# Layer 1's recurrent states two at a time: four row tiles for the spreads, four column tiles for the sums, the decay's second product on two row tiles

## The chip, the cores and the metric

The kernel runs on one core of one Trainium2 chip. The metric is the device time of one execution in microseconds. Two terms are used throughout. A *tile* of TensorE is a rectangle of its 128 by 128 array: a product with 32 input rows needs a row tile of 32 rows, a product with 32 output columns a column tile of 32 columns, and products on different tiles can be issued one right behind the other. A *bank* is a 128 by 512 f32 piece of PSUM, where matmuls leave their results.

## The reference

The input is 32 sequences of 64 tokens with 256 features, in f32. Four layers follow one another: layer 0 is a transformer block with self-attention and cross-attention, layer 1 a recurrent block, layer 2 two cross-attentions with 16 heads of 128 and a bias key and value, then an MLP, layer 3 a cross-attention and an MLP. The change concerns layer 1. It has 32 heads of 8 channels; each head keeps an 8 by 8 state, so that each of the 256 channels i has 8 states j:

```
w = exp(-exp(time_decay + tanh(xw @ td_w1) @ td_w2))     # td_w1: 256x64, td_w2: 64x256
r, k, v = xr @ Wr.T, xk @ Wk.T, xv @ Wv.T
for each token t:
    a      = k[t, i] * v[t, j]
    out[j] = sum over i of r[t, i] * (u[i] * a + s[i, j])
    s      = a + w[t, i] * s
```

What comes out is normalised head by head, multiplied by a gate, and passed through Wo onto the residual.

## The kernel before, in words

The 2048 tokens are cut into four groups g of 512 (8 sequences). Activations stand with features on the partitions: a work tile of `big` is 128 x 2 x 512, the 2 being the halves c of the 256 features. There are 12 such work tiles in rotation.

Each layer is a generator that yields between steps. `weave` runs one as the main thread and lets others advance at a given rate, and a scheduler orders each engine's instructions by priority, which follows the order in which the program issues them. Layer 1 of group 0 runs as the main thread, with layer 0 of group 1 and the precomputed keys and values of layer 2 (`keep`) beside it. Layer 1 of groups 1, 2 and 3 runs as the side thread of `layer2(0)`, `layer2(1)` and `layer2(2)`. In the profile, the state passes of the four groups lie at 313 to 418, 573 to 631, 1005 to 1063 and 1445 to 1501 us.

PSUM is divided in two pools. `bank` hands out 4 single banks. `banks` hands out 2 double banks (128 x 2 x 512, tag b2), which five users share: the spreads `vj`, layer 0's and 3's scores `sp` (L269), layer 2's scores `s2p` (L796), the mixing products `mp` (L488) and the group norm's `gm` and `gv` (L611, L617).

**The states.** The 16 states (c, j) of a group are done two j at a time in eight passes (c, n), where n stands for the states j0 and j0 + 2 with j0 = 0, 4, 1, 5. One pass is `states(c, n)`:

1. Spread (L558): a product with a 0/1 matrix, 32 rows to 128, copies v's channel j of each head to all 8 channels i. Two products, on row tiles m = j // 2, fill one double bank `vj`.
2. Multiply (L567, VectorE): a = vj * k, shifted by a token; GpSimd puts the starting state in front (L563).
3. Two scans (L573, VectorE): s = w * s + a along the tokens.
4. Multiply by r (L574, GpSimd).
5. Sums (L596): a product with another 0/1 matrix, 128 rows to 32 columns, adds up the 8 channels of each head, on two column tiles m of the bank `op`.

The list `ahead` keeps two passes in flight: pass at + 2 is started before the sums of pass at are issued. After the fourth pass of a half, `bp` (L603) adds the part with u. `gm` and `gv` then do the group norm, `og` (L618 to L627) the rest of it, and `al_d` the output product.

**The decay.** `dwp` (L165) multiplies xw by the 64 columns of td_w1, ScalarE takes the tanh on 64 partitions (L505), and two products `wp` (L510), one for each half c, read it; each is followed by two Exps on ScalarE.

`beside(i)` raises the priority of the second of two small products by 4000, so that the scheduler puts it right behind the first.

Names of other work that appears around the states: `al_o` (L331) is layer 2's output product and reads `o` (L836), which VectorE takes from the attention products `pv` (L825); `tp` (L810) are transposes of the softmax weights `pn` (L804, GpSimd); `q2p` (L165) are layer 2's queries; `x` (L344) is the residual; `nt_e` (L190) transposes the norm that follows layer 1's output product.

Of the kernel before, what the change touches and what calls it, by code (L numbers as in the profile page):

```python
# [10 lines left out]
AF = mybir.ActivationFunctionType  # L11
# [3 lines left out]
P = 128  # L15
# [6 lines left out]
NC = D // P  # L22
# [5 lines left out]
C_ID, C_HB, C_HB8, C_SEL, C_GAT, C_M0, C_M1 = 0, 128, 256, 384, 640, 704, 705  # L28
# [40 lines left out]
def kernel(  # L69
# [25 lines left out]
    def bank(name):  # L95
        return psum1.tile([P, 512], F32, tag="b1", name=name)

    def banks(name):
        return psum2.tile([P, 2, 512], F32, tag="b2", name=name)
# [17 lines left out]
    ct = cp.tile([P, C_N], F32, name="ct")  # L117
# [13 lines left out]
    def vec(name, i=0):  # L131
        at = VAT[name] + i
        return vt[:, at : at + 1]
# [27 lines left out]
    def linear(ps, w, at, step, y, cols=P):  # L161

        for kc in range(NC):
            o = at + kc * step
            PE.matmul(ps, w[:, o : o + cols], y[:, kc, :], start=(kc == 0), stop=(kc == NC - 1))  # L165
# [259 lines left out]
    @contextmanager  # L425
    def beside(i):

        if i:
            with tc.high_priority(offset=4000):
                yield  # L430
        else:
            yield
# [5 lines left out]
    def cbt(ap):  # L438

        return ap.rearrange("p c (b t) -> p (c b) t", b=GB)  # L440
# [7 lines left out]
    def layer1(g, work):  # L448
# [50 lines left out]
        yield  # L499
        yield  # L500
        de = big("de")
        dw = de[:64, 0, :]
        ps = bank(f"dwp_{g}")
        linear(ps[:64, :], w5, 384, 64, xw, cols=64)
        A.activation(dw, ps[:64, :], AF.Tanh)  # L505
        ws = big("ws")
        PL.memset(cbt(ws)[:, :, 0:1], 0.0)
        for c in range(NC):
            ps = bank(f"wp_{g}_{c}")
            PE.matmul(ps, w5[:64, 512 + c * P : 512 + (c + 1) * P], dw, start=True, stop=True)  # L510
            e = de[:, 1, :]
            A.activation(e, ps, AF.Exp, bias=vec("L1_xattn_time_decay", c))
            A.activation(bt(ws[:, c, :])[:, :, 1:], bt(e)[:, :, :-1], AF.Exp, scale=-1.0)
        yield

# [31 lines left out]
        yield  # L547
        k, v, r = made["k"], made["v"], made["r"]

        def states(c, n):  # L550

            j0 = (0, 4, 1, 5)[n]
            vj = banks(f"vj_{g}_{c}_{n}")
            for i in range(2):
                m, q = (j0 + 2 * i) // 2, j0 % 2
                rows = slice(32 * m, 32 * m + 32)
                with beside(i):
                    PE.matmul(  # L558
                        vj[:, i, :], ct[rows, C_SEL + q * P : C_SEL + (q + 1) * P], v[rows, c, :],
                        start=True, stop=True,  # L560
                    )
            a = big(f"a{c}{n}")
            PL.tensor_copy(  # L563
                a.rearrange("p i (b t) -> p i b t", b=GB)[:, :, :, 0:1],
                s0t[:, c, j0 : j0 + 3 : 2, g * GB : (g + 1) * GB].unsqueeze(3),
            )
            V.tensor_tensor(  # L567
                a.rearrange("p i (b t) -> p i b t", b=GB)[:, :, :, 1:],
                vj.rearrange("p i (b t) -> p i b t", b=GB)[:, :, :, :-1],
                bt(k[:, c, :])[:, :, :-1].unsqueeze(1).to_broadcast([P, 2, GB, S - 1]), ALU.mult,  # L570
            )
            for i in range(2):
                V.tensor_tensor_scan(a[:, i, :], ws[:, c, :], a[:, i, :], 0.0, ALU.mult, ALU.add)  # L573
            PL.tensor_tensor(a, a, r[:, c : c + 1, :].to_broadcast([P, 2, GT]), ALU.mult)  # L574
            return j0, a

        ruk = big("ruk")
        todo = [(c, n) for c in range(NC) for n in range(4)]
        ahead = [states(*todo[0])]
        yield  # L580
        ahead.append(states(*todo[1]))
        yield
        for c in range(NC):
            V.scalar_tensor_tensor(ruk[:, c, :], r[:, c, :], vec("L1_xattn_u", c), k[:, c, :], ALU.mult, ALU.mult)
        w9 = slot(L1_AT + 4)
        for at, (c, n) in enumerate(todo):
            if at + 2 < 8:
                ahead.append(states(*todo[at + 2]))
                yield
            if n == 0:  # L590
                op = bank(f"op_{g}_{c}")
            j0, a = ahead.pop(0)
            for i in range(2):
                m, q = (j0 + 2 * i) // 2, j0 % 2
                with beside(i):
                    PE.matmul(  # L596
                        op[32 * m : 32 * m + 32, :], ct[:, C_GAT + 32 * q : C_GAT + 32 * q + 32], a[:, i, :],
                        start=(q == 0), stop=(q == 1),
                    )
            yield  # L600
            if n == 3:
                bp = bank(f"bp_{g}_{c}")
                PE.matmul(bp, hb, ruk[:, c, :], start=True, stop=True)  # L603
                V.tensor_tensor(v[:, c, :], bp, v[:, c, :], ALU.mult)
                V.tensor_tensor(v[:, c, :], op, v[:, c, :], ALU.add)
                yield
# [390 lines left out]
def _layout(inputs):  # L997

    import numpy as np

    f = {k: np.asarray(v) for k, v in inputs.items()}
    i = np.arange(D)
    turned = (i // P) * P + (i % 16) * 8 + (i % P) // 16

    def rows(w):

        return w.reshape(-1, P, w.shape[1]).transpose(1, 0, 2).reshape(P, -1)

    def tall(w):

        return np.concatenate([w, np.zeros((P - w.shape[0], w.shape[1]), w.dtype)], 0)

    def slot(*parts):
        w = np.concatenate(parts, 1)
        return np.concatenate([w, np.zeros((P, WSLOT - w.shape[1]), w.dtype)], 1)

    l0 = {k[9:]: v for k, v in f.items() if k.startswith("L0_xattn_")}
    l1 = {k[9:]: v for k, v in f.items() if k.startswith("L1_xattn_")}
    l2 = {k[9:]: v for k, v in f.items() if k.startswith("L2_xattn_")}
    l3 = {k[9:]: v for k, v in f.items() if k.startswith("L3_xattn_")}  # L1020

    def mlp(w1, w2):

        return [slot(rows(w1[:, :512])), slot(rows(w1[:, 512:])), slot(rows(w2[:512])), slot(rows(w2[512:]))]

    qkv, kv = l0["w_qkv"], l0["w_kv"]
    w2 = l1["maa_w2"]
    maa_w1 = np.concatenate([l1["maa_w1"], l1["maa_w1"][:, 128:]], 1)
    slots = [
        slot(rows(qkv[:, :512])),  # L1030
        slot(rows(qkv[:, 512:]), rows(l0["w_ao"])),
        slot(rows(l0["w_q"]), rows(kv[:, :D])),
        slot(rows(kv[:, D:]), rows(l0["w_co"])),
        *mlp(l0["w1"], l0["w2"]),
        slot(rows(maa_w1), rows(l1["td_w1"]), tall(l1["td_w2"])),
        slot(w2[:4].reshape(P, D), tall(np.concatenate([w2[4], w2[4]], 0))),
        slot(rows(l1["Wk"].T), rows(l1["Wv"].T[:, turned])),
        slot(rows(l1["Wr"].T), rows(l1["Wg"].T[:, turned])),
        slot(rows(l1["Wo"].T[turned]), rows(l1["Wfk"].T)),
        slot(rows(l1["Wfr"].T), rows(l1["Wfv"].T)),  # L1040
    ]
    for a in "12":
        for q in range(4):
            at = slice(512 * q, 512 * q + 512)
            slots += [slot(rows(l2[n + a][:, at])) for n in ("wq", "wk", "wv")]
            slots.append(slot(rows(l2["wo" + a][at])))
    slots += mlp(l2["w_fc1"], l2["w_fc2"])
    slots += [
        slot(rows(l3["q_w"]), rows(l3["k_w"])),
        slot(rows(l3["v_w"]), rows(l3["cproj_w"])),  # L1050
        *mlp(l3["fc_w"], l3["proj_w"]),
    ]
    f["L1_xattn_gn_w"] = l1["gn_w"][turned]
    f["L1_xattn_gn_b"] = l1["gn_b"][turned]

    def feature_major(x):

        return x.reshape(G, GT, NC, P).transpose(3, 0, 2, 1)

    def token_major(x):  # L1060

        return x.reshape(G, TT, P, D).transpose(2, 0, 1, 3)

    ctx = f["ctx_2048"]
    arrays = {
        "x": token_major(f["x"]),
        "cT": feature_major(ctx),
        "s0": ctx[:, 2:10].reshape(B, NC, P, 8).transpose(2, 1, 3, 0),
        "m_self": f["mask_1x1xSxS2_fc1"].reshape(S, S),
        "m_cross": f["mask_Bx1xSxS2_ff1"].reshape(B // 2, 2, S, S).transpose(2, 1, 0, 3),  # L1070
        "m_key": np.ascontiguousarray(f["mask_BxS2_bf1"]).view(np.uint8).reshape(B // 2, 2, S).transpose(1, 0, 2),
        "vecs": np.concatenate([f[n].reshape(-1, P).T for n, _ in VECS], 1),
        "brow": np.concatenate([f[n].reshape(-1) for n in ROWS])[None],
        "vrow": np.stack([np.stack([l2[f"b{v}"].reshape(-1), l2[f"bias_v{a}"].reshape(-1)]) for a, v in (("1", "v1"), ("2", "v2"))]),
        "wts": np.stack(slots),
        "cst": _constants(),
    }
    return {k: np.ascontiguousarray(v) for k, v in arrays.items()}
# [27 lines left out]
```

## Time and profile before

| | |
|---|---|
| median of 3 runs | 2191.03 us (2188.73 to 2194.2) |
| the profiled execution | 2198.33 us |
| its span, first to last instruction | 2196.6 us |
| granted TensorE clock, mean | 0.973 |
| TensorE matmul (PE) busy | 2058.2 us, 94% |
| TensorE weight load (PEld) | 1243.4 us, 57% |
| VectorE (DVE) | 1156.9 us, 53% |
| ScalarE (ACT) | 631.8 us, 29% |
| GpSimd (POOL) | 542.4 us, 25% |

The busy times are shares of the span. A line such as `L596 PE MATMUL op<-a,ct 128*32 128x512 f32 x128 | 33.8, 606 | 5.9 <-POOL a L574 5.9` names the program's line, the engine, output and inputs, the tile of the array (rows * columns), the streamed operand, how many records there are, then busy time in us and the mean of one in ns, and last the idle time of the engine just before such an instruction with what ended it. Matmuls are pipelined, so that the length of one record is not what it costs; the distance between starts is. L-numbers are those of the kernel before; in the changed one, lines from L558 on stand up to 16 lower.

### The profile page before, as it was taken

The numbers are of one execution on the slowest core, as the hardware profiler recorded it, in microseconds if no ns is written. First come the engines' busy times: TensorE is split into PE (matmuls) and PEld (weight loads), VectorE is DVE, ScalarE is ACT, GpSimd is POOL, SyncE is SP. The second block draws the span as 40 slices with busy tenths as digits, with TensorE's granted clock in tenths as the row PEclk, the third lists the DMA queues.
The fourth block names the chain that finished last, engine by engine and source line by source line (L and its number), as shares of the span: only waits on it lengthen the run. The fifth ranks groups of instructions, "written<-read, shape, count | busy, mean of one in ns | idle before, by whom it ended". The sixth has DMA issues, their size and how long they took to land. (4 is left out here: it accounts for less than half of the span.)

```text
span 2196.6 us, 36396 instructions
## 1 busy us (share of the span) xinstructions
PE 2058.2 (94%) x15264; PEld 1243.4 (57%) x15264; DVE 1156.9 (53%) x1965; ACT 631.8 (29%) x1000; POOL 542.4 (25%) x498
## 2 busy tenths in 40 slices
PE   5989998999989899999898999999999999999998
PEld 3455444464545565655555656555566767566665
DVE  3672668434655747325548573376574366424662
ACT  1222322223232313232313232322323133321441
POOL 2221344113432313123323131243211111100110
PEclk9999998999999999999999999999999999999998
DMA  7233231237312112333121132331312432212010
GB/s 245 95 128 109 93 104 57 99 106 252 112 58 63 58 47 77 95 112 116 49 63 60 50 100 83 117 123 51 89 55 95 128 121 70 94 43 87 25 39 20
DMA packets 79795, 197.26 MB, mean 90 GB/s; under 512 B 9616, under 2 KB 14352, under 8 KB 79632
## 3 DMA queue, kind: packets, MB, share of 16 engines
q1 hardware_dynamic: 77472, 191.88, 27.2%
q8 instruction: 121, 1.98, 0.4%
q0 software_dynamic: 576, 2.10, 0.3%
q10 hardware_dynamic: 1584, 0.95, 0.1%
q14 instruction: 42, 0.34, 0.1%
HBM read 158.98 MB, written 35.91 MB: 89 GB/s over the span
## 5 line engine op out<-in xcount | busy, mean ns | idle before, releaser
L165 PE MATMUL q2p<-h,w 128*128 128x512 f32 x512 | 245.5, 613 | 7.1 <-DMA w<-in_wts 3.2
L331 PE MATMUL al_o<-w,o 128*128 128x256 f32 x1024 | 235.6, 388 | 11.7 <-DVE o L836 10.7
L331 PEld LDWEIGHTS al_o<-w,o 128*128 128x128 f32 x1024 | 196.9, 194 | 53.3 <-issue 17.6
L786 ACT ACTIVATE q<-q2p,vt 128x512 f32<-128x512 f32 x128 | 87.3, 685 | 284.1 <-PE q2p L165 281.6
L165 PEld LDWEIGHTS q2p<-h,w 128*128 128x128 f32 x512 | 95.4, 194 | 123.0 <-issue 104.9
L804 POOL TENSOR_TENSOR pn<-s,sm 128x512 f32<-128x512 f32 x64 | 72.3, 1132 | 288.9 <-DVE sm L209 206.6
L165 PE MATMUL k2p_f<-c,w 128*128 128x512 f32 x256 | 130.0, 629 | 5.3 <-DMA w<-in_wts 3.3
L734 PE MATMUL v2p_f<-w,c 128*128 128x512 f32 x256 | 122.8, 602 | 0.0
L734 PE MATMUL v2p<-w,c 128*128 128x512 f32 x256 | 118.1, 604 | 2.4 <-ACT pt_b L290 1.3
L165 PE MATMUL k2p<-c,w 128*128 128x512 f32 x256 | 120.0, 593 | 0.0
L945 DVE TENSOR_TENSOR fv<-v2p_f,vb 128x512 f32<-128x512 f32 x64 | 43.8, 686 | 114.9 <-PE v2p_f L734 114.9
L574 POOL TENSOR_TENSOR a<-a,r 128x1024 f32<-128x1024 f32 x32 | 75.7, 2366 | 113.2 <-DVE a L573 99.9
L344 DVE TENSOR_TENSOR x<-al_o,x 128x512 f32<-128x512 f32 x64 | 43.7, 684 | 100.4 <-PE al_o L331 100.4
L836 DVE TENSOR_SCALAR o<-pv,vt 128x256 f32<-128x256 f32 x128 | 55.8, 473 | 74.9 <-PE pv L825 74.6
L936 ACT ACTIVATE fk<-k2p_f,vt 128x512 f32<-128x512 f32 x64 | 44.0, 687 | 172.1 <-PE k2p_f L165 142.1
L772 DVE TENSOR_SCALAR k<-k2p,vt 128x512 f32<-128x512 f32 x64 | 47.3, 744 | 86.3 <-PE k2p L165 86.3
L796 PEld LDWEIGHTS s2p<-k,q 128*64 128x64 f32 x2048 | 67.9, 138 | 42.4 <-issue 30.5
L825 PEld LDWEIGHTS pv<-pt,v 64*64 64x64 f32 x4096 | 72.7, 140 | 26.1 <-issue 17.7
L734 PEld LDWEIGHTS v2p_f<-w,c 128*128 128x128 f32 x256 | 50.1, 196 | 63.8 <-issue 62.4
L200 DVE TENSOR_REDUCE mx<-s2p 128x8 f32<-128x520 f32 x64 | 44.4, 694 | 78.2 <-PE s2p L796 78.0
L825 PE MATMUL pv<-pt,v 64*64 64x64 f32 x4096 | 81.6, 226 | 3.2 <-issue 1.4
L165 PEld LDWEIGHTS k2p<-c,w 128*128 128x128 f32 x256 | 48.9, 191 | 61.3 <-issue 57.9
(310 smaller groups left out, 3733.3 us busy)
## 6 DMA issues: line engine op xcount, KB each, us to landing
w<-in_wts SPq DMA_DIRECT2D x200, 512.0 KB, 3.6
kd<-fk SPq DMA_DIRECT2D x64, 260.0 KB, 2.1
k<-kd SPq DMA_DIRECT2D x64, 260.0 KB, 3.9
vd<-fv SPq DMA_DIRECT2D x64, 256.0 KB, 2.0
v<-vd SPq DMA_DIRECT2D x64, 256.0 KB, 4.3
vb<-in_vrow SPq DMA_DIRECT2D x20, 256.0 KB, 4.1
vs<-in_vrow SPq DMA_DIRECT2D x20, 256.0 KB, 3.4
c<-in_cT POOLq DMA_DIRECT2D x4, 512.0 KB, 11.6
```

The lines of the kernel that those rows point to most:

```text
L165: PE.matmul(ps, w[:, o : o + cols], y[:, kc, :], start=(kc == 0), stop=(kc == NC - 1))
L200: V.tensor_reduce(mx, src, AX.X, ALU.max)
L331: PE.matmul(ps[:, a, :], y[kc][:, i * P : (i + 1) * P], wk[:, o : o + D], start=(kc == 0), stop=(kc == k - 1),)
L574: PL.tensor_tensor(a, a, r[:, c : c + 1, :].to_broadcast([P, 2, GT]), ALU.mult)
L734: PE.matmul(ps, cs[g][:, kc, bp * P : (bp + 1) * P], wv[:, 512 * kc : 512 * kc + 512], start=(kc == 0), stop=(kc == NC - 1),)
L772: V.tensor_scalar_add(k[:, :, :S], bt(ps), vec(f"L2_xattn_bk{a}", hd))
L786: A.activation(q, ps, AF.Identity, bias=vec(f"L2_xattn_bq{a}", hd))
L796: PE.matmul(sp[64 * h2 : 64 * h2 + 64, b // 4, (b % 4) * (S + 1) : (b % 4 + 1) * (S + 1)], qs[h2][:, b * S : (b + 1) * S], ks[h2][:, b, :] ...
L804: PL.tensor_tensor(pn, s[:, :, :S], rc.unsqueeze(2).to_broadcast([P, GB, S]), ALU.mult)
L825: PE.matmul(pv[b2][rows, to : to + S], vals[bp][half, hc : hc + 64], pt[half, bp, h2 * S : (h2 + 1) * S], start=True, stop=True,)
L836: V.tensor_scalar_add(ov[:, :, 1, :], src[1], bv)
L936: A.activation(k[:, :, :S], bt(ps), AF.Identity, bias=vec("L2_xattn_bk1", hd))
```

## The change

The spreads of two passes are issued together by a new function `spread(c, q)`. It takes both double banks, and issues four products on the four row tiles m, one right after another; m = 0 and 1 fill the first bank pair, m = 2 and 3 the second. The multiply, scans and multiply by r stay as they were, one double bank at a time. The sums of two passes are issued together too, on four column tiles of `op`. The yields in the loop stay the same in number.

In the decay, td_w1 is laid out twice side by side, so that `dwp` gives 128 columns and the tanh runs on 128 partitions with two equal halves. td_w2 is packed with its half c = 0 on rows 0 to 63 and c = 1 on rows 64 to 127, and the two `wp` products run on the two row tiles, one right behind the other, each into its own bank; the Exps follow.

```diff
-        dw = de[:64, 0, :]
+        dw = de[:, 0, :]
         ps = bank(f"dwp_{g}")
-        linear(ps[:64, :], w5, 384, 64, xw, cols=64)
-        A.activation(dw, ps[:64, :], AF.Tanh)
+        linear(ps, w5, 384, P, xw)
+        A.activation(dw, ps, AF.Tanh)
         ws = big("ws")
         PL.memset(cbt(ws)[:, :, 0:1], 0.0)
-        for c in range(NC):
-            ps = bank(f"wp_{g}_{c}")
-            PE.matmul(ps, w5[:64, 512 + c * P : 512 + (c + 1) * P], dw, start=True, stop=True)
+        wps = [bank(f"wp_{g}_{c}") for c in range(NC)]
+        for c in range(NC):
+            rows = slice(64 * c, 64 * c + 64)
+            with beside(c):
+                PE.matmul(wps[c], w5[rows, 640 : 640 + P], dw[rows], start=True, stop=True)
+        for c in range(NC):
             e = de[:, 1, :]
-            A.activation(e, ps, AF.Exp, bias=vec("L1_xattn_time_decay", c))
+            A.activation(e, wps[c], AF.Exp, bias=vec("L1_xattn_time_decay", c))
...
-        def states(c, n):
+        def spread(c, q):
+
+            vjs = [banks(f"vj_{g}_{c}_{q}{n}") for n in range(2)]
+
+            def one(m):
+                rows = slice(32 * m, 32 * m + 32)
+                return PE.matmul(
+                    vjs[m // 2][:, m % 2, :], ct[rows, C_SEL + q * P : C_SEL + (q + 1) * P], v[rows, c, :],
+                    start=True, stop=True,
+                )
+
+            last = one(3)
+            with tc.issue_after(last.ins), beside(1):
+                for m in range(3):
+                    one(m)
+            return vjs
+
+        def states(c, n, vj):
 
             j0 = (0, 4, 1, 5)[n]
-            vj = banks(f"vj_{g}_{c}_{n}")
-            for i in range(2):
-                m, q = (j0 + 2 * i) // 2, j0 % 2
-                rows = slice(32 * m, 32 * m + 32)
-                with beside(i):
-                    PE.matmul(
-                        vj[:, i, :], ct[rows, C_SEL + q * P : C_SEL + (q + 1) * P], v[rows, c, :],
-                        start=True, stop=True,
-                    )
...
-        ahead = [states(*todo[0])]
-        yield
-        ahead.append(states(*todo[1]))
+        vjs = spread(0, 0)
+        ahead = [states(*todo[0], vjs[0])]
+        yield
+        ahead.append(states(*todo[1], vjs[1]))
         yield
...
-        for at, (c, n) in enumerate(todo):
-            if at + 2 < 8:
-                ahead.append(states(*todo[at + 2]))
+        for at in range(0, 8, 2):
+            c, q = todo[at][0], at // 2 % 2
+            if at < 6:
+                vjs = spread(todo[at + 2][0], (at // 2 + 1) % 2)
+            for nxt, vj in zip(todo[at + 2 : at + 4], vjs):
+                ahead.append(states(*nxt, vj))
                 yield
-            if n == 0:
+            if q == 0:
                 op = bank(f"op_{g}_{c}")
-            j0, a = ahead.pop(0)
-            for i in range(2):
-                m, q = (j0 + 2 * i) // 2, j0 % 2
-                with beside(i):
+            two = [ahead.pop(0)[1] for _ in range(2)]
+            for m in range(4):
+                with beside(m):
                     PE.matmul(
-                        op[32 * m : 32 * m + 32, :], ct[:, C_GAT + 32 * q : C_GAT + 32 * q + 32], a[:, i, :],
-                        start=(q == 0), stop=(q == 1),
+                        op[32 * m : 32 * m + 32, :], ct[:, C_GAT + 32 * q : C_GAT + 32 * q + 32],
+                        two[m // 2][:, m % 2, :], start=(q == 0), stop=(q == 1),
                     )
             yield
-            if n == 3:
+            if q == 0:
+                yield
+            else:
                 bp = bank(f"bp_{g}_{c}")
...
     maa_w1 = np.concatenate([l1["maa_w1"], l1["maa_w1"][:, 128:]], 1)
+    td_w1 = np.concatenate([l1["td_w1"], l1["td_w1"]], 1)
...
-        slot(rows(maa_w1), rows(l1["td_w1"]), tall(l1["td_w2"])),
+        slot(rows(maa_w1), rows(td_w1), l1["td_w2"].reshape(64, NC, P).transpose(1, 0, 2).reshape(P, P)),
```

In the text, a *quad* is such a burst of four products on four tiles, a *pair* one of two.

## The prediction

> **What bounds the kernel now.** I first read the page: part 1, then the PE and clock rows of part 2.
>
> ```profile
> PE 2058.2 (94%) x15264; PEld 1243.4 (57%) x15264; DVE 1156.9 (53%) x1965; ACT 631.8 (29%) x1000; POOL 542.4 (25%) x498
> PE   5989998999989899999898999999999999999998
> PEclk9999998999999999999999999999999999999998
> ```
>
> TensorE is busy for 2058.2 of 2196.6 us, so it stands still for only 138. Time comes off if matmul time comes off, and only where no new wait takes its place. The second view is the groups by line on PE, for the four that the change touches.
>
> ```profile
> L596 PE MATMUL op<-a,ct 128*32 128x512 f32 x128 | 33.8, 606 | 5.9 <-POOL a L574 5.9
> L558 PE MATMUL vj<-v,ct 32*128 32x512 f32 x128 | 33.0, 640 | 0.0
> L510 PE MATMUL wp<-de,w 64*128 64x512 f32 x16 | 8.7, 667 | 2.3 <-ACT de L505 2.1
> L165 PE MATMUL dwp<-xm,w 128*64 128x512 f32 x16 | 7.7, 605 | 0.6 <-POOL xm L495 0.6
> ```
>
> Each f32 product appears as two passes, so 128 records are 64 products or 32 pairs. Third, the timeline of group 1's states: start, length, engine, line, count, and in brackets the idle time before.
>
> ```profile
> 573.80 1.13 PE L558 MATMUL vj<-v,ct 32*128 32x512 f32 x4
> 574.86 7.17 PE L331 MATMUL al_o<-w,o 128*128 128x256 f32 x32
> 581.97 1.14 PE L558 MATMUL vj<-v,ct 32*128 32x512 f32 x8
> 583.04 0.66 PE L810 MATMUL tp<-ct,pn 128*128 128x128 f32 x4
> 583.62 1.05 PE L596 MATMUL op<-a,ct 128*32 128x512 f32 x4
> 584.61 0.66 PE L810 MATMUL tp<-ct,pn 128*128 128x128 f32 x4
> ...
> 592.36 1.10 PE L331 MATMUL al_o<-w,o 128*128 128x256 f32 x4 [0.90 <-PE vj L558]
> 596.64 5.59 PE L331 MATMUL al_o<-w,o 128*128 128x256 f32 x17 [3.18 <-DVE o L836]
> ```
>
> Here lies the strongest evidence for the change: at 581.97 two spreads happened to stand in a row, and their eight passes took 1.14 us, as long as the four passes at 573.80. Four row tiles do run side by side. The last line shows the other side: PE already waits 3.18 us for DVE's `o`, because DVE is full:
>
> ```profile
> 588.00 3.50 DVE L573 TENSOR_TENSOR_SCAN a<-ws,a 128x512 f32<-128x512 f32 x2
> 591.41 0.84 DVE L836 TENSOR_SCALAR o<-pv,vt 128x256 f32<-128x256 f32 x2
> 592.18 1.19 DVE L567 TENSOR_TENSOR a<-vj,k 128x1008 f32<-128x1008 f32 x1
> 593.47 2.64 DVE L573 TENSOR_TENSOR_SCAN a<-ws,a 128x512 f32<-128x512 f32 x2
> ```
>
> The stage windows (columns: stretch, length, busy us and count of PE, PEld, DVE, ACT, POOL, then clock) tell how much room each group has:
>
> ```profile
> 573.00:640.00 67.00, 59.97 (x501) 33.31 (x498) 45.49 (x54) 13.82 (x24) 26.01 (x16) 0.95 0.29 87
> 312.00:430.00 118.00, 107.99 (x546) 50.30 (x545) 81.90 (x103) 28.68 (x45) 41.14 (x36) 0.94 0.23 83
> 1440.00:1510.00 70.00, 67.62 (x713) 36.90 (x713) 50.88 (x64) 20.17 (x35) 25.86 (x16) 1.00 0.29 92
> ```
>
> Group 1 (and group 2, at 1005, with 59.96) idles 7 of 67 us; group 0 10 of 118; group 3 2.4 of 70.
>
> **What is saved on PE.** A spread pair costs 1.06 us from its first start to the next matmul (574.86 - 573.80) and about 0.09 more on the pass ahead of it (0.52 to the next start at a change of tile shape, where a plain 128x512 pass takes 0.43): 1.15. Three of the 32 pairs already merge as at 581.97, so there are 29 bursts and will be 16: 13 x 1.15 = 14.9 us. A sums pair costs 584.61 - 583.62 = 0.99, and 0.09 ahead: 1.08. 32 bursts become 16: 17.3 us. That four column tiles run at once no 512-wide row shows; the nearest rows are the sums' own two and `pv_b` (L298), whose four tiles start 7 ns apart. I take the two-tile length; were they in sequence, the 17.3 would be nearly nothing. `wp` runs two products in sequence, 1.91 us from first start to the next matmul, against 1.06 for a pair side by side: 4 x 0.85 = 3.4. `dwp` grows from 64 to 128 columns, which costs nothing (605 ns a pass against 593 to 629 for full tiles) and loses its change of shape, 4 x 0.1 = 0.4. ACT's tanh over 128 rows instead of 64 and its two Exps keep their free size of 512, so I cost them at nothing. In all 14.9 + 17.3 + 3.8 = 36.0 us: 3.8 in the decay, 8.9 in group 0 (eight pairs and eight sums) and 7.8 in each other group (one pair there is merged already).
>
> **What is added: waits.** All of them follow from one fact: a spread used one of two double banks (tag b2) and now takes both, which `sp` (L269), `s2p` (L796), `mp`, `gm` and `gv` share. What lies between two quads doesn't grow, but both multiplies of one must be done before the next, and DVE issues two multiplies (1.20 each), then four scans (1.2 to 1.5 each) without the old chance to slip something between. The row for the bank is the multiply itself, 1.20 after the burst; the rule stands behind it. The Trainium skill, "TensorEngine Tiling (Array Packing)", section "Gotcha 1: PSUM Pressure", says that row tiling raises the pressure on PSUM, since different row tiles go to different banks; it speaks against this change, and gives no price. No row of before has a quad that waits for a bank; by the rows above each such wait lies between 0 and the two multiplies, 2.4 us.
>
> Group 1, along the changed program's order. The first quad stands behind `s2p` of the other chain, whose max and subtract (0.70 us each) hold the second bank until 575.4; two tiles go at 573.8, two wait, and `al_o` begins at 576.5 instead of 574.9: +1.6. The next quad is clear. The third follows after eight transposes (1.2 us), while both multiplies need until 587.1: +1.3. The next `al_o` waits for four `o` pieces, now behind up to seven scans and two multiplies: DVE reaches the first two at 596.3 and the last at 600.8; the remaining 28 passes take 6.2 and one half-clock stretch like that of before (there the clock row reads 0.53 from 596.9 to 600.5) 1.7, so it ends at 608.3, against 604.5. That is +3.8 with all savings so far counted in. Behind it two spread bursts (2.3) and three sums bursts (3.2) are still saved: -5.5. The last sums need both products of POOL (2.37 each), where before two lay apart: +1.5. `al_d`, which waits 2.7 us for POOL's `og` (L627), has less work ahead of it, but the wait behind it, 1.9 at `nt_e`, goes: +0.8. Sum +0.6, and the same for group 2.
>
> Group 3: -7.8; waits for a DVE subtract 1.1, an x add 0.7, another subtract 1.3, POOL's `pn` 2.2, and the last POOL product 2.0: -0.5. Group 0: -8.9; the second quad waits for both multiplies (+1.5), `qp_b1_0` for a normalisation `y_b` behind scans (+2.0), the third quad for a DVE mask multiply of `sp_b` (+3.2): -2.2 if they all stay, -8.9 if its 10 us of old idle absorb them; I take the middle, -5.5.
>
> Total: -5.5 + 0.6 + 0.6 - 0.5 - 3.8 = -8.6. The profiled execution took 2198.33 us, so 2189.7; times 2191.03 / 2198.33, the median over that execution, 2182.4.
>
> **Bounds.** If no wait appears: -36.0, so 2155. If in group 0 all stay (+3.3) and each group suffers two more half-clock stretches of 1.7 us (+13.6): +8.3, so 2199.
>
> **Rivals.**
> *A, the matmul time comes through.* The waits of before absorb the new ones, or DVE catches up. For: PE is 94% busy and the merged bursts are real. Against: the 3.18 us row shows DVE late in that very place. -36 to -20: 2155 to 2171, drawn at 2163. Chance 0.13.
> *B, slower: the double banks.* Place: groups 1 and 2 between the first quad and the last `al_o` of the states. If each quad waits a full two multiplies (2.4) and holds back `s2p`, then the other chain's softmax comes late too, and a stall of over about 1.5 us is followed by a half-clock stretch. Price: six quads after the first in groups 1 and 2 at 2.4 + 1.7 less what is already in the sum (some 8): +16, that is 2191 - 8.6 + 16 = 2198, or with the same in group 3 and 0 2205. It decides as soon as the stalls exceed 8 us a group. For: 0.90 us before `al_o` at 592.36 was already a wait in the shadow of a spread. Chance 0.26.
> *C, no change.* Four column tiles run in sequence, so that the 17.3 falls away. Where PE would have waited anyway, that costs nothing, elsewhere all of it: between -8.6 and -8.6 + 17.3 = +8.7, the middle 0.0, so 2191. For: no row shows four 512-wide column tiles. Against: the row tiles did merge. Chance 0.15.
> My forecast case (-20 to -2) has 0.46.
>
> **Numbers.** What differs by under 0.3% (6.6 us) can't be told from no change. Faster by more (below 2184.5): 0.34 of the forecast case and all of A, 0.47. Same: 0.12 of the forecast and nearly all of C, 0.25. Slower: B and a sliver of C, 0.28. The range 2160 to 2203 leaves out about half of A and a third of B.
>
> **What would show it.** Right: L558's group shows quads of eight passes in some 0.55 us of starts, `op` four tiles within 10 ns, PE busy down by some 30 us, and its idle time up by 20 or more, under the names of DVE `a` (the multiply), DVE `o` and POOL `a`. Wrong: idle time as before (then A), or PE busy down by only 15 (then C), or new waits at `s2p` and many clock dips in groups 1 and 2 (then B).

## The result, and the profile after

The changed kernel takes 2233.03 us (median of 6 runs, 2224.65 to 2234.86), the kernel before 2191.84 in the same comparison: ratio 1.0181, 95% interval 1.0164 to 1.0199. It is 41 us slower, where 2182.4 was forecast and the range ended at 2203.

First the page of the changed kernel: part 1, then the PE and clock rows of part 2.

```profile
span 2222.9 us, 36429 instructions
PE 2036.9 (92%) x15264; PEld 1235.7 (56%) x15264; DVE 1170.2 (53%) x1965; ACT 637.0 (29%) x1006; POOL 549.7 (25%) x498
PE   6989898999779899997899999989999899999998
PEclk9999999999889999998999999989999999999999
```

TensorE's busy time fell from 2058.2 to 2036.9 us, by 21. The span grew by 26, so that the time in which TensorE stands still went from 138 to 186: +48. (The two profiled executions lie 26 us apart and the medians 41: the profiled one of before, 2198.33, is a long one of its kernel, that of the change, 2224.65, the shortest of its six.) The groups on PE for the four products:

```profile
L610 PE MATMUL op<-a,ct 128*32 128x512 f32 x128 | 21.2, 630 | 12.6 <-POOL a L585 8.4 <-DVE x L344 4.2
L559 PE MATMUL vj<-v,ct 32*128 32x512 f32 x128 | 29.9, 680 | 5.6 <-DVE s L205 3.0 <-DVE s_b L389 1.4 <-DVE a L578 1.1
L512 PE MATMUL wp<-de,w 64*128 64x512 f32 x16 | 4.5, 641 | 2.2 <-ACT de L505 2.2
L165 PE MATMUL dwp<-xm,w 128*128 128x512 f32 x16 | 7.6, 599 | 0.6 <-POOL xm L495 0.6
```

The sums fell from 33.8 to 21.2 us and `wp` from 8.7 to 4.5. The spreads only went from 33.0 to 29.9. The timeline of group 1's states says why; first TensorE, then VectorE.

```profile
559.47 1.13 PE L559 MATMUL vj<-v,ct 32*128 32x512 f32 x4
561.19 1.13 PE L559 MATMUL vj<-v,ct 32*128 32x512 f32 x4 [0.60 <-DVE s L205]
562.25 7.17 PE L331 MATMUL al_o<-w,o 128*128 128x256 f32 x32
569.35 1.14 PE L559 MATMUL vj<-v,ct 32*128 32x512 f32 x8
...
571.82 2.25 PE L559 MATMUL vj<-v,ct 32*128 32x512 f32 x8 [0.31 <-DVE a L578]
574.00 1.16 PE L841 MATMUL pv<-pt,v 64*64 64x64 f32 x64
575.09 1.06 PE L610 MATMUL op<-a,ct 128*32 128x512 f32 x8
576.09 1.17 PE L841 MATMUL pv<-pt,v 64*64 64x64 f32 x64
584.91 2.04 PE L331 MATMUL al_o<-w,o 128*128 128x256 f32 x4 [7.65 <-issue]
590.80 8.95 PE L331 MATMUL al_o<-w,o 128*128 128x256 f32 x28 [3.84 <-DVE o L852]
```

```profile
572.80 7.66 DVE L584 TENSOR_TENSOR_SCAN a<-ws,a 128x512 f32<-128x512 f32 x4
580.39 2.29 DVE L578 TENSOR_TENSOR a<-vj,k 128x1008 f32<-128x1008 f32 x2
582.60 1.44 DVE L584 TENSOR_TENSOR_SCAN a<-ws,a 128x512 f32<-128x512 f32 x1
583.97 0.84 DVE L852 TENSOR_SCALAR o<-pv,vt 128x256 f32<-128x256 f32 x2
584.73 5.54 DVE L584 TENSOR_TENSOR_SCAN a<-ws,a 128x512 f32<-128x512 f32 x3
590.20 0.84 DVE L852 TENSOR_SCALAR o<-pv,vt 128x256 f32<-128x256 f32 x2
```

Eight passes of the sums take 1.06 us, as four did: four column tiles run side by side. The second quad takes 1.14, as forecast. But the first comes in two pieces, and the third, with 0.31 us of wait, takes 2.25: one of its products starts when the first multiply has left its bank, the other three 1.1 us later, behind the second multiply. Counted over the whole timeline, 7 of the 16 quads run whole and 9 in two pieces, so that 25 bursts stand where before had 29.

The dear place is `al_o`: TensorE stands for 7.65 and 3.84 us where before it stood for 0.90 and 3.18 (the profile names no releaser for the 7.65; group 2 has the same wait, 7.71 us, under DVE `o`). The 28 passes behind take 8.95 us, at a half clock for part of it. VectorE's four scans in a row take 7.66 us, and three take 5.54: not 1.2 each. The stage window over these waits (columns as in the prediction) shows how long the clock stayed low, 17.1 us, where the stretch of before at 597.1 us lasted 3.4:

```profile
579.10:596.20 17.10, 7.45 (x17) 5.48 (x18) 11.94 (x11) 0.00 (x0) 9.36 (x6) 0.50 0.13 46
```

The waits of TensorE, the largest that the change made or enlarged (us in all, times, longest); first the longest of them as before had it, then the changed kernel:

```profile
PE al_o L331 <- DVE o L836: 10.7, 5, 3.2
```

```profile
PE al_o L331 <- DVE o L852: 18.6, 5, 7.7
PE op L610 <- POOL a L585: 8.4, 4, 2.5
PE h_h L165 <- DVE hm L192: 8.1, 3, 6.8
PE v2p L750 <- DVE k L788: 8.0, 2, 4.5
PE al_o L331 <- issue: 7.7, 1, 7.7
```

Two of them (`h_h`, an MLP product of layer 2, and `v2p`, a product of layer 2's values) are far from any state pass. They led to the second half of the cause.

**A correction to the description of the change.** It says that the yields in the loop stay the same in number. They do not. Before, a group's states yield once for every pass started, once for every pass summed and once after each `bp`: with the two ahead of the loop that is 2 + 6 + 8 + 2 = 18. After, each turn of the loop yields for two passes started, once for the sums, and once more, either for `bp` or instead of it: 2 + 6 + 4 + 4 = 16. Layer 1 is a thread in a weave, and two yields fewer let it and everything behind it in its thread run ahead of the other thread.

### The profile page after: what moved, and what is told of

Read it like the earlier page. It is cut to its first block, busy times and chain, and to the rows that moved or that the text cites. A ratio compares the mean times of both kernels' runs of the same rounds, so it can differ in the third digit from the quotient of the medians.

```text
span 2222.9 us, 36429 instructions
## 1 busy us (share of the span) xinstructions
PE 2036.9 (92%) x15264; PEld 1235.7 (56%) x15264; DVE 1170.2 (53%) x1965; ACT 637.0 (29%) x1006; POOL 549.7 (25%) x498
## 5 line engine op out<-in xcount | busy, mean ns | idle before, releaser
L750 PE MATMUL v2p<-w,c 128*128 128x512 f32 x256 | 122.6, 619 | 9.6 <-DVE k L788 8.0
L584 DVE TENSOR_TENSOR_SCAN a<-ws,a 128x512 f32<-128x512 f32 x64 | 102.8, 1651 | 0.2
L585 POOL TENSOR_TENSOR a<-a,r 128x1024 f32<-128x1024 f32 x32 | 83.8, 2621 | 69.0 <-DVE a L584 64.7
```

Source lines behind the costliest of these rows:

```text
L750: PE.matmul(ps, cs[g][:, kc, bp * P : (bp + 1) * P], wv[:, 512 * kc : 512 * kc + 512], start=(kc == 0), stop=(kc == NC - 1),)
```

## Experiments

All ratios are against the kernel before in the same comparison (its medians there were 2193.7 to 2194.7 us).

| run | spreads | sums | yields | median us | ratio, 95% interval | less before |
|---|---|---|---|---|---|---|
| the change | fours | fours | 16 | 2233.03 | 1.0181 (1.0164 to 1.0199) | +41.2 |
| e1_yields18 | fours | fours | 18 | 2208.16 | 1.0062 (1.0041 to 1.0083) | +14.4 |
| e2_before16 | pairs | pairs | 16 | 2218.46 | 1.0113 (1.0093 to 1.0132) | +24.7 |
| e9_before16_g3 | pairs | pairs | 16 in group 3 | 2216.17 | 1.0096 (1.0080 to 1.0112) | +21.5 |
| e3_decay | pairs | pairs | 18 | 2190.29 | 0.9984 (0.9971 to 0.9997) | -3.5 |
| e4_sums4 | pairs | fours | 18 | 2179.60 | 0.9933 (0.9917 to 0.9949) | -14.1 |
| e6_decay_sums4 | pairs | fours | 18 | 2180.06 | 0.9935 (0.9920 to 0.9950) | -14.3 |
| e10_ds4_16_g012 | pairs | fours | 16 in groups 0 to 2 | 2180.65 | 0.9936 (0.9923 to 0.9949) | -14.1 |
| e5_spread4 | fours | pairs | 18 | 2218.89 | 1.0114 (1.0099 to 1.0128) | +24.6 |
| e7_quads_no_r | fours | fours | 18 | 2182.40 | 0.9946 (0.9933 to 0.9958) | -11.9 |
| e8_before_no_r | pairs | pairs | 18 | 2180.64 | 0.9936 (0.9922 to 0.9950) | -13.7 |
| e11_quads_r_dve | fours | fours | 18 | 2198.97 | 1.0021 (1.0004 to 1.0038) | +4.3 |
| e12_quads_r_late | fours | fours | 18 | 2201.19 | 1.0030 (1.0019 to 1.0041) | +6.5 |

The change, e1, e3, e6, e7, e10, e11 and e12 have the decay's part of the change; the others have not.

**The yields, from both sides.** The changed kernel with two yields more, and the kernel before with two fewer:

```diff
# e1_yields18, against the changed kernel
             yield
-            if q == 0:
-                yield
-            else:
+            yield
+            if q == 1:
                 bp = bank(f"bp_{g}_{c}")
# e2_before16, against the kernel before
-            yield
-            if n == 3:
+            if n != 3:
+                yield
+            else:
                 bp = bank(f"bp_{g}_{c}")
```

> The changed kernel with one yield more in each half of the states, so that layer 1 again yields 18 times there as before, not 16. Theory 1 (the two lost yields let the light thread run ahead of the main one, and all work behind is woven anew; that is the loss): about 2183 us (2165 to 2195), which is the sum of the prediction without the reweaving. Theory 2 (the quads on both double banks stall PE): it stays at 2225 to 2235.

> The kernel before, unchanged in its products, with 16 yields in the states: the sums of the fourth pass and the bp step share one. Theory 1 (reweaving): slower by 35 to 55 us, 2225 to 2245, with no quad in it. Theory 2 (double banks): within 5 us of before, 2187 to 2197.

Neither run landed in a stated range: e1 lies between those of its two theories, and so does e2. The 16 yields alone cost 24.7 us, the rest of the change at 18 yields 14.4. The sum is 39.1, the whole change costs 41.2: the two parts account for it and add up within their intervals. The waits of e2 show what the shift does without any quad:

```profile
PE v2p L735 <- DVE k L773: 8.2, 2, 4.6
PE h_h L165 <- DVE hm L192: 8.1, 3, 6.8
```

They are the two waits of the changed kernel that lay far from the states; the trace of before has neither of them under these names. The place of the longest, in the timeline of TensorE; first before, then e2:

```profile
1717.62 1.04 PE L190 MATMUL nt_h<-ct,xn_h 128*128 128x128 f32 x8
1718.50 7.07 PE L331 MATMUL al_j<-w,hm_j 128*128 128x256 f32 x32
1725.41 7.89 PE L165 MATMUL h_h<-hm,w 128*128 128x512 f32 x18
```

```profile
1724.73 6.64 PE L331 MATMUL al_j<-w,hm_j 128*128 128x256 f32 x30
1731.20 1.04 PE L190 MATMUL nt_h<-ct,xn_h 128*128 128x128 f32 x8
1739.05 7.41 PE L165 MATMUL h_h<-hm,w 128*128 128x512 f32 x11 [6.81 <-DVE hm L192]
```

After the transposes `nt_h`, layer 2's MLP waits for VectorE's norm. Before, layer 3's last product `al_j` of group 0 stood just there and filled the 7 us. With two yields fewer the light thread is ahead, `al_j` is done too soon, and nothing is left to fill the gap.

**Which group's yields.**

```diff
# e9_before16_g3, against the kernel before
-            yield
+            if n != 3 or g != 3:
+                yield
             if n == 3:
```

> The kernel before with the two yields taken out in group 3 alone. If the reweaving's whole loss arises where the light thread (layer 1 of group 3, then layer 3 of group 0) runs out before layer 2 of group 2 is done, as the 16-yield run's late stalls say: +18 to +28 us, 2212 to 2222. If every group pays its share: a quarter to a third, +6 to +8, about 2201.

+21.5 of the 24.7 us: most of the loss arises in group 3's weave. Its trace has the same wait of `h_h`, and behind the states of group 3, between 1500 and 1760 us, two more that before does not have:

```profile
PE h_h L165 <- DVE hm L192: 6.8, 1, 6.8
PE tp_i L289 <- DVE s_i L279: 3.9, 1, 3.9
PE h_j L165 <- ACT hm_j L352: 2.1, 1, 2.1
```

Together they are 12.8 us; in the whole trace TensorE's idle time is 13.0 us longer than before (151.4 against 138.4). `h_j` waits for ScalarE's `hm_j`, which stands there behind an Exp of layer 2 (L206) and two loads of function tables of 1.28 us each. The other wait of e2, `v2p`, belongs to groups 1 and 2, and e9 has none of it.

**The parts one by one, at 18 yields.**

```diff
# e4_sums4, against the kernel before (in the loop over the passes)
+            if n % 2 == 1:
+                q = n // 2
+                two = [ahead.pop(0)[1] for _ in range(2)]
+                for m in range(4):
+                    with beside(m):
+                        PE.matmul(op[32 * m : 32 * m + 32, :], ..., two[m // 2][:, m % 2, :], ...)
```

e3_decay is the decay's part of the diff alone, e5_spread4 the function `spread` with the sums in pairs, e6_decay_sums4 e3 and e4 together.

> The kernel before with the decay's part of the change alone (dwp on 128 columns, wp on two row tiles); the order on every engine stays. By the prediction's sum -3.8 us: 2188. If the late first Exp costs as much as the pair saves: 2191 to 2192.

> The kernel before with the sums alone in fours, issued at every second pass, and 18 yields; the spreads stay in pairs on one double bank. If four column tiles run side by side, 16 bursts of 1.08 us go: 2174 to 2182 (-17 less some 0 to 8 for waits on the second product). If they run in sequence: 2189 to 2193, and the bursts' starts spread over twice the time.

> Spreads alone in fours on both double banks, with 18 yields, sums in pairs and the decay as before. If the parts add up, the 18-yield kernel's +14.4 us less the sums' -14.1 and the decay's -3.5 leaves +32: about 2225, with some 106 us of scans where before has 84. If the sums in fours were part of the loss (they wait for the second of two products), less: about 2210.

> Before with the sums in fours and the decay on two row tiles, spreads in pairs, 18 yields. If the two gains add: -17.6 us, 2176 (2172 to 2180). If the sums already gave back what the decay gains: 2179.

The sums in fours bring 14.1 us, and part 1 of the page shows it cleanly: TensorE's busy time falls by 21.0 in the profiled execution, and its span by 22.4 (2174.2), so that no idle time comes back. (The profiled executions flatter it, 22.4 us apart where the medians are 14.1: they are the longest of before and the shortest of e4. The row of the sums falls from 33.8 to 22.3 us; 12 of the 16 quads run whole.)

```profile
PE 2037.2 (94%) x15264; PEld 1238.4 (57%) x15264; DVE 1157.3 (53%) x1965; ACT 631.7 (29%) x1000; POOL 542.4 (25%) x498
```

The decay's part brings 3.5 alone (the interval reaches nearly to nothing) and nothing that can be told on top of the sums. The spreads in fours cost 24.6. Adding up the parts would have left +32 for them, or 28.7 if the sums and the decay count together as e6 measured them; the intervals do not tell 28.7 from 24.6. In the page of e5, TensorE's busy time hardly falls (first line); the second line is the row of its spreads:

```profile
PE 2054.8 (93%) x15264; PEld 1243.2 (56%) x15264; DVE 1176.4 (53%) x1965; ACT 631.8 (29%) x1000; POOL 547.4 (25%) x498
L556 PE MATMUL vj<-v,ct 32*128 32x512 f32 x128 | 27.6, 647 | 3.6 <-DVE s_b L389 1.3 <-DVE s L205 1.2 <-DVE a L575 1.1
```

It falls by 5.4 us (33.0 to 27.6) and not by the 14.9 of the sum, because 8 of its 16 quads run in two pieces: 24 bursts in place of 29, not 16. The granted clock, 0.968 on the mean against 0.973, takes some of that back: the sums, which e5 leaves as they were, take 35.1 us in place of 33.8. Idle time is 159.6 against 138.4 us.

**Why spreads in fours cost.** The rows of VectorE's scans: before, then the changed kernel (columns: busy us, mean ns).

```profile
L573 DVE TENSOR_TENSOR_SCAN a<-ws,a 128x512 f32<-128x512 f32 x64 | 82.4, 1318 | 1.7
```

```profile
L584 DVE TENSOR_TENSOR_SCAN a<-ws,a 128x512 f32<-128x512 f32 x64 | 102.8, 1651 | 0.2
```

64 scans take 20 us more. The timeline of e1 shows beside what; two scans on VectorE, then GpSimd:

```profile
585.31 1.19 DVE L584 TENSOR_TENSOR_SCAN a<-ws,a 128x512 f32<-128x512 f32 x1
586.43 3.29 DVE L584 TENSOR_TENSOR_SCAN a<-ws,a 128x512 f32<-128x512 f32 x1
```

```profile
585.54 3.11 POOL L585 TENSOR_TENSOR a<-a,r 128x1024 f32<-128x1024 f32 x1 [2.34 <-DVE a L584]
589.87 2.35 POOL L585 TENSOR_TENSOR a<-a,r 128x1024 f32<-128x1024 f32 x1 [1.22 <-DVE a L584]
...
595.28 3.17 POOL L585 TENSOR_TENSOR a<-a,r 128x1024 f32<-128x1024 f32 x1 [1.84 <-DVE a L584]
```

GpSimd's multiply by r of the first state begins when its two scans are done, and the two scans of the second state follow on VectorE at once. One of them then takes 3.29 us: wherever a scan in e1 takes that long (9 of 64), it lies beside this multiply for 2.2 us. The Trainium skill, "SBUF — State Buffer", section "Who interferes with whom", says that a VectorE instruction with two SBUF inputs contends with a GpSimd instruction that reads SBUF, and that the order of issue decides which of them blocks. The trace agrees: the scan at 585.31 was there first and keeps its 1.19 us, GpSimd's multiply behind it takes 3.11 in place of 2.35 and ends at 588.64; the scan at 586.43 comes second and ends 1.08 us after that. The multiply L578 (one input from PSUM) is not held up, as the durations in e1 show (shortest, median and longest, in ns):

```profile
L584 DVE TENSOR_TENSOR_SCAN a<-ws,a x64: 1160/1210/3314, 313.6 to 1501.1; 128x512 f32<-128x512 f32 x64
L578 DVE TENSOR_TENSOR a<-vj,k x32: 1174/1194/1208, 311.4 to 1496.6; 128x1008 f32<-128x1008 f32 x32
```

Two runs leave the multiply by r out, and two move it:

```diff
# e7_quads_no_r against e1; e8_before_no_r the same against the kernel before
-            PL.tensor_tensor(a, a, r[:, c : c + 1, :].to_broadcast([P, 2, GT]), ALU.mult)
# e11_quads_r_dve against e1
-            PL.tensor_tensor(a, a, r[...], ALU.mult)
+            V.tensor_tensor(a, a, r[...], ALU.mult)
# e12_quads_r_late against e1: GpSimd's second product of a pair first
-            PL.tensor_tensor(a, a, r[...], ALU.mult)
+            if n % 2 == 0:
+                waiting.append(a)
+            else:
+                times = lambda a: PL.tensor_tensor(a, a, r[...], ALU.mult)
+                with tc.issue_after(times(a).ins):
+                    times(waiting.pop())
```

> The changed kernel with 18 yields, without GpSimd's multiply by r (L574 of before): the sums are taken of the states alone. Contention theory (the scans on VectorE go slow while GpSimd multiplies, and quads put more scans beside it): all scans at 1.2 us, 78 in all in place of 106, PE's wait for o down from 20 us to under 9, time 2165 to 2180. Bank theory (both double banks are held too long by the multiplies): scans don't matter, the wait for o stays at 15 to 20, time 2195 to 2205.

> The kernel before, likewise without GpSimd's multiply by r: the measure for the run above. Scans 84 to 78 us, PE's waits for GpSimd's product (5.9 us) gone: 2181 to 2188. By the contention theory the gap between quads and pairs (+14.4) shrinks to under 0 without this multiply, by the bank theory it stays over +8.

> The 18-yield kernel with quads, the multiply by r moved from GpSimd to VectorE. Contention theory: scans 78 us again, but 32 multiplies of 1.1 to 1.2 us come onto the same engine: 36 more against 28 less, so VectorE's row is about as long and the time stays near 2208 (2198 to 2214). If it was not the shared time but GpSimd's latency that counted: 2190 or less.

> The 18-yield kernel with quads; GpSimd multiplies the second state of a pair first and the first behind it, so that it starts when all four scans are done. All other orders stay. Contention theory: scans fall from 106 to under 90 us, PE's wait for o from 20 to 9 to 13, the sums wait some 2 us longer each: 2193 to 2202. Bank theory: the sums' waits alone are new, 2208 to 2220.

Without the multiply, quads (2182.4) and pairs (2180.6) are level: the gap shrinks from 14.4 to 1.8 us, so this multiply stands behind some 12 of the 14 (the intervals leave each gap uncertain by 4 to 5 us). e7 lies 2.4 us above the range of the contention theory and 13 below that of the bank theory; its wait for `o`, 11.6 us, is not under 9 as the first had said. Scans are short again (e7):

```profile
L584 DVE TENSOR_TENSOR_SCAN a<-ws,a 128x512 f32<-128x512 f32 x64 | 76.6, 1245 | 0.2
```

These two runs also take away what the sums wait for on GpSimd, so they do not isolate the contention. e12 does: it changes nothing but the order of GpSimd's queue (in the traces the order of instructions on TensorE, VectorE and ScalarE is that of e1), the products are all there, and although the sums now wait longer for GpSimd (10.2 us in all against 7.7), the time falls from +14.4 to +6.5 with scans of

```profile
L586 DVE TENSOR_TENSOR_SCAN a<-ws,a 128x512 f32<-128x512 f32 x64 | 87.1, 1407 | 0.2
```

So the contention is shown for some 8 of the 14.4 us; e12 removes it only in part, since two of its scans still take 3.3, and its wait for `o` (15.3 us) falls less than expected. With r on VectorE (e11) the time is +4.3, at the lower edge of the range that was given, with short scans (77.5 us) and 32 multiplies more on VectorE.

What stays: even in e7 TensorE's busy time is 25.6 us lower than in e8 and the time is not. Its idle time is 25 us longer, 146.3 against 121.4; `al_o` waits 4.31 and 1.74 us in group 1, where it has 0.66 and 2.88 in e8. How much of that is the bank and how much VectorE doing two multiplies and four scans in one piece, no run tells apart.

**A faster version.** Pairs for the spreads and fours for the sums win 0.67% (e4). The early marks of the 16-yield run suggested more for 16 yields in groups 0 to 2:

```diff
# e10_ds4_16_g012, against e6
-            yield
+            if n != 3 or g == 3:
+                yield
```

> Sums in fours and the decay's part, spreads in pairs, 16 yields in groups 0, 1 and 2 but 18 in group 3. In the 16-yield run all marks up to group 3 stood some 4 to 8 us early. If that is real: 2172 to 2176, below the 2180 of the same parts with 18 yields. If groups 0 to 2 pay too: 2183 to 2190.

It gives nothing more and lies between its two ranges: 2180.65 against 2180.06. Its trace has `v2p`'s wait too (7.6 us in all), so that wait costs nothing on balance. Standing early in the middle of a span was not worth anything at its end.

## Why the prediction was wrong

*The step that failed first is one that the sum does not have:* what the change does to the order of all the work behind it. The prediction took the order of instructions near the states from the changed program, but took for granted that the rest kept its place, on the premise that the yields stay the same in number; it put nothing down for it. Two yields of 18 cost 24.7 of the 41 us, 21.5 of it in the weave of group 3 and `layer2(2)`, up to 250 us after the states, where `h_h`, `tp_i` and `h_j` now wait. No rival names it: B spoke of banks and of groups 1 and 2.

*The second is a term that was mis-sized:* the scans at "1.2 to 1.5 each". The prediction showed a row with two scans in 3.50 us (at 588.00, beside GpSimd's multiply by r), so that one of them took over 2, and priced none above 1.5. They take up to 3.3. So the `o` pieces came later than it said: VectorE was to reach the first two 22.5 us after the first quad's start (596.3 - 573.8) and the last 27.0 us after it; it reached them after 24.5 (583.97 - 559.47) and 30.7 us, and `al_o` went on after 25.4 and 31.3. Behind the last of them a half-clock stretch of 3.4 us was priced; the trace has one of 17.1 us, whose last 5.4 fall on these passes. The prediction's sum by groups, against the marks of e1 (the start of the same ScalarE instruction ahead of and behind each group's states, e1 less before):

| | predicted | marks in e1 |
|---|---|---|
| group 0 | -5.5 | -3.4 to -4.9: -1.5 |
| group 1 | +0.6 | -5.1 to +3.0: +8.1 |
| group 2 | +0.6 | -1.2 to +4.8: +6.0 |
| group 3 | -0.5 | +4.8 to +12.2: +7.4 |

The marks add up to +20.0; what lies between the groups gives some of it back (-3.4 ahead of group 0, -4.2 between groups 1 and 2), and the span of e1 is 12.7 us longer. One slip in the sum is small beside this: 600.8 + 6.2 + 1.7 is 608.7 and not 608.3, which makes groups 1 and 2 0.4 us dearer each.

*What was right:* what a whole burst saves. Four row tiles take 1.14 us as two do, four column tiles 1.06; the sums' 17.3 came as 14.1, the decay's 3.8 as 3.5 alone. The spreads' 14.9 did not come: their row fell by 3.1 us, since 9 of 16 quads ran in two pieces. The sum had booked some of this as waits, and in group 1 it named the right two quads. The direction of the waits was right too: PE busy down by 21 (some 30 was said), idle time up by 48 (20 or more was said) under DVE `o` and POOL `a`. In group 1 the bank costs what was said: 0.6 us at the first quad and 0.31 at the third plus 1.1 each that is lost where the quad falls apart, so 1.7 and 1.4, about the 1.6 and 1.3 put down.

*Rival B* had the sign, and its price, +7 to +14, is near the +14.4 of e1. That is in part luck. Its long half-clock stretches did come (17.1 us in group 1). But what it names as their cause, the double banks, is not the larger part of what the runs show: the scans' contention with GpSimd is, which e12 lowers without touching a bank. Its threshold is not sharp either: in the trace of before, 19 of the 26 stalls over 1.5 us are followed by a half-clock stretch within 3.5 us, one of 1.41 us (at 344.6) is too, and one of 2.74 us (at 653.4) is not. *A* and *C* are refuted by e5 and by the 1.06 us row.

## What to carry to other kernels

Count the yields of a woven thread before and after an edit, or compare the order of the instructions far behind it: two lost yields cost more here than everything the edit did in its own place. Where matmul time comes off, look at who must feed the next product: batching the spreads by four put VectorE's scans beside GpSimd's multiply and the won matmul time came back as idle time, while batching the sums gave no engine more work and brought 14 us. A row whose mean hides two lengths (1.2 and 2.4 us) is a warning that a neighbour matters; price it by the neighbour, not by the mean.

## What the runs showed of the hardware

A VectorE scan of 128x512 f32 takes 1.2 us alone and up to 3.3 beside a GpSimd product of 128x1024, which itself goes from 2.35 to 3.17 when it comes second; with the product left out (e7) or moved to VectorE (e11), 61 of 64 scans take 1.2 us. Four column tiles of 128x512 f32 take 1.06 us, as long as two. And a quad whose products wait for two banks that come free 1.1 us apart runs in two pieces: 2.25 us in place of 1.14.
